# Right taps of layer 2's closing convolutions and feed-forward on VectorE, shifted copies from one plain tile

## The chip, the cores and the metric

The kernel runs as one program on one core of a Trainium2 chip. The metric is the device time of one execution in microseconds. Before the change the median of three runs is 25713.89 us (25709.84 to 25717.19).

## What is computed

The network has four layers on images of 64 channels and 64x64 pixels, batch 8. The parts concerned are in layer 2. Everything is fp32. Its last steps are, cut to what matters:

```python
y = spa_ssm(x0, ...) + x0                                   # selective scan, residual
y = dwconv3x3(gelu(dwconv3x3(y, vout_dw1)), vout_dw2) + y   # the closing convolutions
x = y + x
t = layernorm(x, ln2_g, ln2_b)
t = leaky_relu(conv1x1(t, ff_w1), 0.2)                      # 64 -> 256 channels
t = leaky_relu(dwconv3x3(t, ff_dw), 0.2)                    # depthwise, 256 channels
x = conv1x1(t, ff_w2) + x                                   # 256 -> 64 channels
```

`dwconv3x3` is a depthwise 3x3 convolution with zero padding: each output pixel of a channel is the sum of nine neighbours of the same channel, each by a weight ("tap") of that channel.

## The kernel before

Tiles are bands of 16 image rows: T = 1024 pixels. The closing convolutions (`l2_finish`) have two images on 128 partitions (a pair), NP = 4 pairs and 4 bands in each, so 16 ticks; the feed-forward (`l2_ffn`) has one image at a time, NB = 8, 32 ticks.

A strip is a padded band of 18 rows of 66 pixels for 64 channels. Its lower 64 partitions hold the band from column 1, its upper 64 partitions the same band from column 2, one pixel shifted. So one matmul over 128 partitions with a diagonal weight (`full`) adds the middle and the left tap of one row of the 3x3 window. The right tap is a second matmul over 64 partitions with the weight `right`; `conv_pair` sends the first half of the rows through the lower and the second half through the upper partitions, and two strips (e = 0, 1: two images, or two groups of 64 channels) to the two halves of the output's partitions. In one `conv_pair` there are twelve matmuls for the middle and left taps (L340), twelve for the right ones (L350), and for the second closing convolution four more that add the residual `y` through an identity (L363). The result stands in a PSUM tile of 128x1024.

`tap_diag` (L323) makes the diagonal weights on VectorE at the start of each of the two parts.

In `l2_finish` a tick t runs `fetch(t + 2)`, `first(t)`, `second(t - 1)`, in that order on every queue, as the schedule is by hand. `fetch` (L1394) loads both shifted copies of each image by DMA, half of them issued from SyncE, half from GpSimd. `first` convolves, ScalarE applies gelu for each image into the lower half of strip `mid` (L1411), GpSimd copies it to the upper half (L1412) and takes over two rows from the band before (L1414). `second` convolves `mid`, VectorE adds the layer's input `x` (L1432), and SyncE stores. At the end of an image pair `second` does one more row: GpSimd overwrites rows of `mid` (L1427, L1428) and a small convolution follows.

In `l2_ffn` a tick t convolves four groups of 64 hidden channels in two pairs (`convolve(t, j)`), and between its halves makes the hidden channels of two ticks later (`hidden(t + 2, g)`: a matmul into `pf` at L330, leaky relu by ScalarE at L1578, the shifted copy by VectorE at L1637, edge rows by GpSimd at L1639 and L1640), the norm of three ticks later (`centre`, L1615 and L1617; `scale`, L1622 to L1627) and at its end the output of the tick before (`output(t - 1)`, matmuls at L1663, VectorE's addition `xo` at L1671). The hidden matmul's weight holds each group of 64 columns twice, and only the lower half of `pf` is read. PSUM pool `pf` has one buffer, shared by `hidden` and `output`; `ps` and `pc` have two each.

Of the kernel before, what the change touches and what calls it, by code (L numbers as in the profile page):

```python
# [18 lines left out]
C = 64  # L19
HW = 64  # L20
# [86 lines left out]
def layouts(i):  # L107
# [61 lines left out]

    o["l2_f1"] = twice(np.repeat(i[p + "ff_w1"].reshape(C, 4, 1, C), 2, axis=2).reshape(C, 4, 128))  # L170
    o["l2_fd"] = twice(i[p + "ff_dw"].reshape(9, 4, C).transpose(2, 1, 0))
    o["l2_f2"] = i[p + "ff_w2"].reshape(2, 128, C).transpose(1, 0, 2)

# [75 lines left out]
class Net:  # L249
# [64 lines left out]

    def tap_diag(self, cp, names, w):

        full, right = (cp.tile([128, 3, C], F32, name=x) for x in names)
        for r in range(2):
            at = slice(r * C, r * C + C)
            for i in range(3):  # L320
                for t, j in ((full, 1 - r), (right, 2)):
                    tap = w[at, i * 3 + j : i * 3 + j + 1]
                    self.nc.vector.tensor_scalar(t[at, i, :], self.ident[at, at], tap, None, ALU.mult)  # L323
        return full, right

# [6 lines left out]
    def conv_pair(self, ps, ws, pads, r0, rows=(8, 8), term=None):  # L332


        for h, n in enumerate(rows):
            for i in range(3):
                for e in range(2):
                    o = ps[e * C : e * C + C, h * 512 : h * 512 + n * HW].rearrange("p (a b) -> p a b", b=HW)
                    f = r0 + h * 8 + i
                    self.nc.tensor.matmul(  # L340
                        o, ws[e][0][:, i, :], pads[e][0][:, f : f + n, 1 : HW + 1], start=i == 0, stop=False
                    )
            yield True
        for i in range(3):
            for h, n in enumerate(rows):
                at = slice(h * C, h * C + C)
                for e in range(2):
                    o = ps[e * C : e * C + C, h * 512 : h * 512 + n * HW].rearrange("p (a b) -> p a b", b=HW)
                    f = r0 + h * 8 + i
                    self.nc.tensor.matmul(  # L350
                        o,
                        ws[e][1][at, i, :],
                        pads[e][h][at, f : f + n, 2 : HW + 2],
                        start=False,
                        stop=i == 2 and term is None,
                    )
        if term is not None:
            for h, n in enumerate(rows):
                at = slice(h * C, h * C + C)
                for e in range(2):  # L360
                    o = ps[e * C : e * C + C, h * 512 : h * 512 + n * HW].rearrange("p (a b) -> p a b", b=HW)
                    f = term[1] + h * 8
                    self.nc.tensor.matmul(  # L363
                        o, self.ident2[at, :C], term[0][e][h][at, f : f + n, 1 : HW + 1], start=False, stop=True
                    )
        yield True
# [984 lines left out]
    def l2_finish(self, src, hy, dst):  # L1351
# [3 lines left out]
        with ExitStack() as ctx:  # L1355
# [3 lines left out]
            dw = self.load(cp, "l2_dw")  # L1359
            convs = [self.tap_diag(cp, (f"conv{j}", f"right{j}"), dw[:, j, :]) for j in range(2)]  # L1360

            def rows(name, n):
# [4 lines left out]
                return [[self.padded(t) for t in pair] for pair in flat]  # L1367


            sums, mids = rows("sum", 4), rows("mid", 2)  # L1370
            total = 4 * NP
# [8 lines left out]
            def fetch(t):  # L1380
                if t >= total:
                    return
                q, c = divmod(t, 4)
                lo, hi = max(0, c * 16 - 1), min(HW, c * 16 + 17)
                at = lo - (c * 16 - 1)
                for i in range(2):
                    s = sums[t % 4][i][0]
                    if c == 0:
                        nc.gpsimd.memset(s[:, 0, :], 0.0)
                    if c == 3:  # L1390
                        nc.gpsimd.memset(s[:, 17, :], 0.0)
                    for r in range(2):
                        engine = nc.sync if r else nc.gpsimd
                        engine.dma_start(  # L1394
                            s[r * C : r * C + C, at : at + hi - lo, 1 + r : 1 + r + HW],
                            hy[q, i * C : i * C + C, lo * HW : hi * HW].rearrange("p (a b) -> p a b", b=HW),
                        )
                xs[t] = []
                for r0, _, _, n in parts(c):
                    xs[t].append(tp.tile([128, n * HW], F32, name="x" if n > 1 else "x1"))  # L1400
                    nc.sync.dma_start(xs[t][-1], src[q, :, r0 * HW : (r0 + n) * HW])

            def first(t):
                if t >= total:
                    return
                ps = p1.tile([128, T], F32, name="ps")
                yield from self.conv_pair(ps, (convs[0],) * 2, sums[t % 4], 0)
                for i in range(2):
                    s, last = mids[t % 2][i][0], mids[(t - 1) % 2][i][0]
                    o = s[:C, 2:18, 1 : 1 + HW]  # L1410
                    nc.scalar.activation(o, like(ps[i * C : i * C + C], o), AF.Gelu)  # L1411
                    nc.gpsimd.tensor_copy(s[C:, 2:18, 2 : 2 + HW], o)  # L1412
                    if t % 4:
                        nc.gpsimd.tensor_copy(s[:, 0:2, :], last[:, 16:18, :])  # L1414
                    else:
                        nc.gpsimd.memset(s[:, 1, :], 0.0)

            def second(t):
# [3 lines left out]
                for (r0, m0, s0, n), x in zip(parts(c), xs.pop(t)):  # L1422
                    if n == 1:

                        for i in range(2):
                            s = mids[t % 2][i][0]
                            nc.gpsimd.tensor_copy(s[:, 0:2, :], s[:, 16:18, :])  # L1427
                            nc.gpsimd.memset(s[:, 2, :], 0.0)  # L1428
                    ps = p2.tile([128, T], F32, name="ps")
                    halves = (8, n - 8) if n > 8 else (n,)  # L1430
                    yield from self.conv_pair(ps, (convs[1],) * 2, mids[t % 2], m0 - 1, halves, (sums[t % 4], s0))
                    nc.vector.tensor_tensor(x, ps[:, : n * HW], x, ALU.add)  # L1432
                    nc.sync.dma_start(dst[q, :, r0 * HW : (r0 + n) * HW], x)

            with tc.manual_schedule():
                for t in range(2):
                    fetch(t)
                for t in range(total + 1):
                    fetch(t + 2)
                    for _ in first(t):  # L1440
                        pass
                    for _ in second(t - 1):
                        pass

# [135 lines left out]
    def l2_ffn(self, src, dst):  # L1580
# [6 lines left out]
        with ExitStack() as ctx:  # L1587
# [3 lines left out]
            cent2, mean2 = self.load(cp, "cent2"), self.load(cp, "mean2")  # L1591
            f1, fd, f2, g2, b2 = (self.load(cp, "l2_" + n) for n in ("f1", "fd", "f2", "g2", "b2"))
            w = [self.tap_diag(cp, (f"full{g}", f"right{g}"), fd[:, g, :]) for g in range(4)]
            flat = [[cp.tile([128, 18 * (HW + 2) + 1], F32, name=f"strip{j}{g}") for g in range(4)] for j in range(3)]
            for row in flat:
                for t in row:
# [31 lines left out]

            def hidden(t, g):
                if t >= total:  # L1630
                    return
                c = t % 4
                s, last = strips[t % 3][g][0], strips[(t - 1) % 3][g][0]
                pf = pf_.tile([128, T], F32, name="pf")
                self.sides(pf, f1[:, g, :], xn[t])
                self.leaky(s[:C, 1:17, 1 : HW + 1], pf[:C].rearrange("p (a b) -> p a b", b=HW))
                nc.vector.tensor_copy(s[C:, 1:17, 2 : HW + 2], s[:C, 1:17, 1 : HW + 1])  # L1637
                if c:
                    nc.gpsimd.tensor_copy(s[:, 0, :], last[:, 16, :])  # L1639
                    nc.gpsimd.tensor_copy(last[:, 17, :], s[:, 1, :])  # L1640
                else:
                    nc.gpsimd.memset(s[:, 0, :], 0.0)
                if c == 3:
                    nc.gpsimd.memset(s[:, 17, :], 0.0)

            def convolve(t, j):

                pc = pc_.tile([128, T], F32, name="pc")
                g = slice(2 * j, 2 * j + 2)
                yield from self.conv_pair(pc, w[g], strips[t % 3][g], 0)  # L1650
                h[t, j] = hp.tile([128, T], F32, name=f"h{j}")
                self.leaky(h[t, j], pc)
# [22 lines left out]
            with tc.manual_schedule():  # L1675
# [5 lines left out]
                for t in range(2):  # L1681
                    for g in range(4):
                        hidden(t, g)
                for t in range(total):
                    fetch(t + 4)
                    for j in range(2):
                        more = convolve(t, j)
                        for g in range(2):
                            hidden(t + 2, 2 * j + g)
                            next(more)  # L1690
                        (scale if j else centre)(t + 3)
# [285 lines left out]
```

## Time and profile before

| | us |
|---|---|
| median of the runs | 25713.89 |
| profiled execution | 25708.36 |
| its span, first to last instruction | 25706.6 |
| PE busy | 21763.6 (85%) |
| VectorE busy | 22248.8 (87%) |
| GpSimd busy | 21624.2 (84%) |
| ScalarE busy | 14830.2 (58%) |
| closing convolutions, first to last matmul | 10933.3 to 11213.3 |
| feed-forward, first matmul to last `xo` | 11219.1 to 12219.3 |

The span is the time from the first instruction to the last of one profiled execution; the runs' times contain a little around it. The busy shares are means over stages with different limits (most of the span is selective scans, which the change does not touch), so they do not tell what bounds the two parts concerned. PE, PEld, DVE, ACT and POOL are TensorE's matmuls and weight loads, VectorE, ScalarE and GpSimd. In a row of the timeline the start and the duration in us come first, then engine, line, operation, output and inputs; the bracket is the idle time before it and what ended it. In a row of groups, the numbers after the bar are the total busy us, the mean ns of one instruction, and the idle time before them.

### The profile page before, as it was taken

What the parts mean: (1) busy time and instruction counts of PE and PEld (TensorE: products, weight loads), DVE (VectorE), ACT (ScalarE), POOL (GpSimd) and SP (SyncE); (2) the same over time, 40 slices, a digit from 0 to 9 for tenths busy, and PEclk for the clock granted to TensorE, in tenths of its full rate; (3) what the DMA queues carried; (4) which work ended last, traced back from release to release, by engine and by line L of the source; (5) the groups of instructions that cost most, each with busy time, mean ns of one, the idle gap of its engine ahead of it and who ended that gap; (6) DMA issues with size and microseconds to landing.
All of it is one profiled execution on the core that took longest, in us unless ns stands there. A gap on an engine that the chain in (4) does not pass through costs nothing. (4 is left out here: it accounts for less than half of the span.)

```text
span 25706.6 us, 198113 instructions
## 1 busy us (share of the span) xinstructions
PE 21763.6 (85%) x55754; PEld 8441.0 (33%) x55754; DVE 22248.8 (87%) x12884; ACT 14830.2 (58%) x18642; POOL 21624.2 (84%) x10205
## 2 busy tenths in 40 slices
PE   8777888888888888789888888888878888888888
PEld 5522333333333223222333333333333333333333
DVE  4389989989899689922899999999989999999999
ACT  4345555555555455512666666666666666666666
POOL 0089999999999579910899999999989999999999
PEclk9888999999999999998999999999999999999999
DMA  2289899888888568830555455545545555555554
GB/s 60 79 292 318 311 316 314 309 311 316 309 312 311 186 266 325 308 62 15 161 169 170 166 172 167 170 168 168 169 155 169 168 170 169 169 168 171 167 171 157
DMA packets 1775344, 5292.32 MB, mean 206 GB/s; under 512 B 536720, under 2 KB 543060, under 8 KB 1706400
## 3 DMA queue, kind: packets, MB, share of 16 engines
q1 hardware_dynamic: 1744032, 5207.12, 59.5%
q10 hardware_dynamic: 27136, 63.34, 0.8%
q0 software_dynamic: 3072, 9.18, 0.2%
q8 instruction: 443, 7.26, 0.1%
q14 instruction: 661, 5.41, 0.1%
HBM read 5122.15 MB, written 156.11 MB: 205 GB/s over the span
## 5 line engine op out<-in xcount | busy, mean ns | idle before, releaser
L444 POOL TENSOR_TENSOR hb<-du,bc 128x1024 f32<-128x1024 f32 x4608 | 10746.5, 2356 | 495.5 <-DVE h L460 325.9
L286 PE MATMUL acc<-hc,ident 128*128 128x512 f32 x18816 | 8872.6, 613 | 90.9 <-DVE img L1207 62.3
L451 ACT ACTIVATE dA<-dt,w_A 128x512 f32<-128x512 f32 x8192 | 5662.6, 691 | 4112.6 <-DVE hc L474 3121.8
L460 DVE TENSOR_TENSOR_SCAN dA<-dA,hb 128x1024 f32<-128x1024 f32 x3384 | 7725.6, 2283 | 283.9 <-ACT dA L451 113.0
L286 PE MATMUL acc<-h,ident 128*128 128x512 f32 x7808 | 4557.9, 713 | 2350.0 <-POOL h L474 2349.9
L286 PEld LDWEIGHTS acc<-hc,ident 128*128 128x128 f32 x18816 | 3686.5, 199 | 5290.5 <-issue 4660.2
L444 POOL TENSOR_TENSOR hb<-du,b 128x1024 f32<-128x1024 f32 x2048 | 4869.5, 2403 | 487.7 <-DVE h L460 257.7
L474 DVE TENSOR_TENSOR hc<-dA,bc 128x1024 f32<-128x1024 f32 x3296 | 4035.9, 1224 | 260.5 <-issue 6.3
L451 ACT ACTIVATE dA<-dt,w_l_A 128x1024 f32<-128x1024 f32 x2560 | 2856.4, 1117 | 1178.3 <-DVE hc L474 749.9
L460 DVE TENSOR_TENSOR_SCAN dA<-dA,carry,hb 128x1024 f32<-128x1024 f32 x1320 | 3095.1, 2345 | 167.7 <-ACT carry L1190 109.6
L286 PEld LDWEIGHTS acc<-h,ident 128*128 128x128 f32 x7808 | 1547.8, 216 | 5013.8 <-POOL h L474 3146.0
L460 DVE TENSOR_TENSOR_SCAN h<-dA,hb 128x1024 f32<-128x1024 f32 x1352 | 3082.4, 2280 | 47.0 <-ACT dA L451 46.3
L474 POOL TENSOR_TENSOR h<-h,bc 128x1024 f32<-128x1024 f32 x1312 | 3088.5, 2354 | 14.2 <-DVE h L460 14.2
L474 DVE TENSOR_TENSOR hc<-dA,c 128x1024 f32<-128x1024 f32 x1408 | 1723.9, 1224 | 117.3 <-DMA c<-bc 6.2
L474 POOL TENSOR_TENSOR h<-h,c 128x1024 f32<-128x1024 f32 x640 | 1512.4, 2363 | 10.0 <-ACT carry L1190 9.6
L460 DVE TENSOR_TENSOR_SCAN h<-dA,carry,hb 128x1024 f32<-128x1024 f32 x600 | 1404.7, 2341 | 81.9 <-ACT dA L451 76.4
L451 ACT ACT_TABLE_LOAD x1122 | 1439.5, 1283 | 21.2 <-ACT tmp L976 1.2
L1190 ACT COPY carry<-dA 128x1 f32<-128x1 f32 x1056 | 167.9, 159 | 1746.1 <-DVE hc L474 1681.9
L1844 PE MATMUL mm<-xn,taps 128*128 128x512 f32 x2048 | 938.9, 600 | 33.1 <-POOL xn L1810 30.8
L673 POOL MEMSET xf<- 128x24 f32 x33 | 4.3, 141 | 910.0 <-PE ps L694 732.3
L1859 PE MATMUL mm<-u,w_xp 128*36 128x512 f32 x1024 | 518.9, 631 | 145.2 <-ACT u L1856 140.8
L1640 POOL COPY strip<-strip 128x66 f32<-128x66 f32 x96 | 22.9, 238 | 722.3 <-DVE strip L1637 696.1
(304 smaller groups left out, 19121.0 us busy)
## 6 DMA issues: line engine op xcount, KB each, us to landing
bc<-bc SPq DMA_DIRECT2D x4096, 512.0 KB
b<-bc SPq DMA_DIRECT2D x2048, 512.0 KB
c<-bc SPq DMA_DIRECT2D x2048, 512.0 KB
bc<-bc SPq DMA_DIRECT2D x512, 1024.0 KB
tmp<-rs SPq DMA_DIRECT2D x93, 512.0 KB
raw<-x SPq DMA_DIRECT2D x64, 512.0 KB
inv<-rs SPq DMA_DIRECT2D x64, 512.0 KB
tmp<-x SPq DMA_DIRECT2D x192, 128.0 KB
```

What stands on the lines that cost most here:

```text
L286: self.nc.tensor.matmul(o, lhsT, r, start=start, stop=stop)
L444: nc.gpsimd.tensor_tensor(s.shaped(hb[i]), s.shaped(s.du), B.pop(i), ALU.mult)
L451: nc.scalar.activation(dA[i][:, cut], s.dt[:, cut], AF.Exp, scale=A[:, n : n + 1])
L460: nc.vector.tensor_tensor_scan(h[:, way], dA[i][:, way], hb.pop(i)[:, way], s.first(n), ALU.mult, ALU.add)
L474: engine.tensor_tensor(s.shaped(o), s.shaped(h), CC.pop(i), ALU.mult)
L673: nc.gpsimd.memset(x[:, :, HW:], 0.0)
L1190: nc.scalar.copy(self.carry[:, n : n + 1], h[:, last : last + 1])
L1640: nc.gpsimd.tensor_copy(last[:, 17, :], s[:, 1, :])
L1844: nc.tensor.matmul(tokens(px[:, j * W : j * W + W]), taps[k][:, m, j * 128 : j * 128 + 128], xn[:, :, f : f + HW], start=m == 0, stop=m == 1,)
L1859: nc.tensor.matmul(pd, xp[:, k, j, :], u[:, j * W : j * W + W], start=j == 0, stop=j == 1)
```

## The change

The middle and left taps stay on TensorE. The right taps become three VectorE instructions on the finished PSUM tile (`right_taps`): each multiplies a window of the band by a per-channel weight and adds it to the PSUM tile in place. For that a plain tile holds 128 channels at once (two images, or two groups of hidden channels) without the shift, and GpSimd makes the two strips from it with four copies (`twin`). Weights `right` are no longer made.

In the closing convolutions `fetch` loads the plain tile `sumx` alone, in two DMAs of 128 partitions, both issued from SyncE; `spread(t + 1)` makes strips `sum` from it, one tick ahead, in GpSimd's queue before `first(t)`. There are three pairs of `sum` strips instead of four, and four plain tiles. Gelu runs once on 128 partitions into plain tile `midx`, and `twin` makes strips `mid`. Row copies are done for three tiles instead of two.

In the feed-forward a hidden step makes two groups at once, so two steps in a tick instead of four; leaky relu writes the plain tile, `twin` makes two strips, and VectorE's shifted copy goes. The first half of each convolution is now issued before the hidden step. The scalars for the right taps of two groups are loaded as `l2_fx`.

```diff
-    o["l2_f1"] = twice(np.repeat(i[p + "ff_w1"].reshape(C, 4, 1, C), 2, axis=2).reshape(C, 4, 128))
+    o["l2_f1"] = twice(i[p + "ff_w1"].reshape(C, 2, 128))
+    o["l2_fx"] = i[p + "ff_dw"].reshape(9, 2, 128).transpose(2, 1, 0)
...
+    def right_taps(self, ps, x, w, r0, n):
+        o = ps[:, : n * HW].rearrange("p (a b) -> p a b", b=HW)
+        for i in range(3):
+            self.nc.vector.scalar_tensor_tensor(
+                o, x[:, r0 + i : r0 + i + n, 2 : HW + 2], w[:, 3 * i + 2 : 3 * i + 3], o, ALU.mult, ALU.add
+            )
+
+    def twin(self, pair, x, rows):
+        for e in range(2):
+            v = x[e * C : e * C + C, rows, 1 : HW + 1]
+            for r in range(2):
+                self.nc.gpsimd.tensor_copy(pair[e][0][r * C : r * C + C, rows, 1 + r : 1 + r + HW], v)
...
-        for i in range(3):
+        for i in range(3 if right[0] is not None else 0):
...
-            sums, mids = rows("sum", 4), rows("mid", 2)
+            sums_x, mids_x = plain("sumx", 4), plain("midx", 2)
+            sums, mids = rows("sum", 3), rows("mid", 2)
...
-                    for r in range(2):
-                        engine = nc.sync if r else nc.gpsimd
-                        engine.dma_start(
-                            s[r * C : r * C + C, at : at + hi - lo, 1 + r : 1 + r + HW],
-                            hy[q, i * C : i * C + C, lo * HW : hi * HW].rearrange("p (a b) -> p a b", b=HW),
-                        )
+                for e, f in ((0, 9), (9, 18)):
+                    f0, f1 = max(lo, lo - at + e), min(hi, lo - at + f)
+                    nc.sync.dma_start(
+                        s[:, f0 - lo + at : f1 - lo + at, 1 : 1 + HW],
+                        hy[q, :, f0 * HW : f1 * HW].rearrange("p (a b) -> p a b", b=HW),
+                    )
...
+            def spread(t):
+                if t < total:
+                    self.twin(sums[t % 3], sums_x[t % 4], slice(0, 18))
...
-                for i in range(2):
-                    s, last = mids[t % 2][i][0], mids[(t - 1) % 2][i][0]
-                    o = s[:C, 2:18, 1 : 1 + HW]
-                    nc.scalar.activation(o, like(ps[i * C : i * C + C], o), AF.Gelu)
-                    nc.gpsimd.tensor_copy(s[C:, 2:18, 2 : 2 + HW], o)
+                self.right_taps(ps, sums_x[t % 4], dw[:, 0, :], 0, 16)
+                x = mids_x[t % 2]
+                o = x[:, 2:18, 1 : 1 + HW]
+                nc.scalar.activation(o, like(ps, o), AF.Gelu)
+                for s, last in zip([x] + [m[0] for m in mids[t % 2]], [mids_x[t % 2 - 1]] + [m[0] for m in mids[t % 2 - 1]]):
                     if t % 4:
                         nc.gpsimd.tensor_copy(s[:, 0:2, :], last[:, 16:18, :])
                     else:
                         nc.gpsimd.memset(s[:, 1, :], 0.0)
+                self.twin(mids[t % 2], x, slice(2, 18))
...
-                        for i in range(2):
-                            s = mids[t % 2][i][0]
+                        for s in [mids_x[t % 2]] + [m[0] for m in mids[t % 2]]:
                             nc.gpsimd.tensor_copy(s[:, 0:2, :], s[:, 16:18, :])
                             nc.gpsimd.memset(s[:, 2, :], 0.0)
...
+                    self.right_taps(ps, mids_x[t % 2], dw[:, 1, :], m0 - 1, n)
                     nc.vector.tensor_tensor(x, ps[:, : n * HW], x, ALU.add)
...
                 for t in range(total + 1):
                     fetch(t + 2)
+                    spread(t + 1)
+                    first(t)
+                    second(t - 1)
...
-                self.leaky(s[:C, 1:17, 1 : HW + 1], pf[:C].rearrange("p (a b) -> p a b", b=HW))
-                nc.vector.tensor_copy(s[C:, 1:17, 2 : HW + 2], s[:C, 1:17, 1 : HW + 1])
+                o = v[:, 1:17, 1 : HW + 1]
+                self.leaky(o, like(pf, o))
+                self.twin(pair, v, slice(1, 17))
...
                 yield from self.conv_pair(pc, w[g], strips[t % 3][g], 0)
+                self.right_taps(pc, plain[t % 3][j], fx[:, j, :], 0, 16)
...
                         more = convolve(t, j)
-                        for g in range(2):
-                            hidden(t + 2, 2 * j + g)
-                            next(more)
+                        next(more)
+                        hidden(t + 2, j)
+                        next(more)
                         (scale if j else centre)(t + 3)
```

More of the change, by code (lines that the diff above doesn't have):

```diff
@@ L313, in folded, with tap_diag @@
         return full, right
-    def tap_diag(self, cp, names, w):
-        full, right = (cp.tile([128, 3, C], F32, name=x) for x in names)
+    def tap_diag(self, cp, name, w):
+        t = cp.tile([128, 3, C], F32, name=name)
         for r in range(2):
@@ L320, in tap_diag @@
             for i in range(3):
[L321 to L324, printed above, removed]
+                tap = w[at, i * 3 + 1 - r : i * 3 + 2 - r]
+                self.nc.vector.tensor_scalar(t[at, i, :], self.ident[at, at], tap, None, ALU.mult)
+        return t
+    def right_taps(self, ps, x, w, r0, n):
[9 more added lines that the diff above has]
+                self.nc.gpsimd.tensor_copy(pair[e][0][r * C : r * C + C, rows, 1 + r : 1 + r + HW], v)
     def sides(self, ps, lhsT, rhs, start=True, stop=True):
@@ L332, in conv_pair @@
     def conv_pair(self, ps, ws, pads, r0, rows=(8, 8), term=None):
+        full, right = zip(*ws)
         for h, n in enumerate(rows):
@@ L340, in conv_pair @@
                     self.nc.tensor.matmul(
-                        o, ws[e][0][:, i, :], pads[e][0][:, f : f + n, 1 : HW + 1], start=i == 0, stop=False
+                        o,
+                        full[e][:, i, :],
+                        pads[e][0][:, f : f + n, 1 : HW + 1],
+                        start=i == 0,
+                        stop=i == 2 and right[e] is None and term is None,
                     )
             yield True
-        for i in range(3):
+        for i in range(3 if right[0] is not None else 0):
             for h, n in enumerate(rows):
@@ L351, in conv_pair @@
                         o,
-                        ws[e][1][at, i, :],
+                        right[e][at, i, :],
                         pads[e][h][at, f : f + n, 2 : HW + 2],
@@ L1359, in l2_finish @@
             dw = self.load(cp, "l2_dw")
-            convs = [self.tap_diag(cp, (f"conv{j}", f"right{j}"), dw[:, j, :]) for j in range(2)]
+            convs = [(self.tap_diag(cp, f"conv{j}", dw[:, j, :]), None) for j in range(2)]
             def rows(name, n):
@@ L1367, in rows, with plain @@
                 return [[self.padded(t) for t in pair] for pair in flat]
-            sums, mids = rows("sum", 4), rows("mid", 2)
+            def plain(name, n):
+                flat = [cp.tile([128, 18, HW + 2], F32, name=f"{name}{j}") for j in range(n)]
+                for t in flat:
+                    nc.gpsimd.memset(t, 0.0)
+                return flat
+            sums_x, mids_x = plain("sumx", 4), plain("midx", 2)
+            sums, mids = rows("sum", 3), rows("mid", 2)
             total = 4 * NP
@@ L1385, in fetch @@
                 at = lo - (c * 16 - 1)
-                for i in range(2):
[L1387 to L1391, printed above, removed]
-                    for r in range(2):
-                        engine = nc.sync if r else nc.gpsimd
-                        engine.dma_start(
-                            s[r * C : r * C + C, at : at + hi - lo, 1 + r : 1 + r + HW],
-                            hy[q, i * C : i * C + C, lo * HW : hi * HW].rearrange("p (a b) -> p a b", b=HW),
-                        )
+                s = sums_x[t % 4]
+                if c == 0:
+                    nc.gpsimd.memset(s[:, 0, :], 0.0)
+                if c == 3:
+                    nc.gpsimd.memset(s[:, 17, :], 0.0)
+                for e, f in ((0, 9), (9, 18)):
[4 more added lines that the diff above has]
+                    )
                 xs[t] = []
@@ L1406, in first @@
                 ps = p1.tile([128, T], F32, name="ps")
-                yield from self.conv_pair(ps, (convs[0],) * 2, sums[t % 4], 0)
-                for i in range(2):
-                    s, last = mids[t % 2][i][0], mids[(t - 1) % 2][i][0]
-                    o = s[:C, 2:18, 1 : 1 + HW]
-                    nc.scalar.activation(o, like(ps[i * C : i * C + C], o), AF.Gelu)
-                    nc.gpsimd.tensor_copy(s[C:, 2:18, 2 : 2 + HW], o)
+                for _ in self.conv_pair(ps, (convs[0],) * 2, sums[t % 3], 0):
+                    pass
+                self.right_taps(ps, sums_x[t % 4], dw[:, 0, :], 0, 16)
[3 more added lines that the diff above has]
+                for s, last in zip([x] + [m[0] for m in mids[t % 2]], [mids_x[t % 2 - 1]] + [m[0] for m in mids[t % 2 - 1]]):
                     if t % 4:
@@ L1423, in second @@
                     if n == 1:
-                        for i in range(2):
-                            s = mids[t % 2][i][0]
+                        for s in [mids_x[t % 2]] + [m[0] for m in mids[t % 2]]:
                             nc.gpsimd.tensor_copy(s[:, 0:2, :], s[:, 16:18, :])
@@ L1430, in second @@
                     halves = (8, n - 8) if n > 8 else (n,)
-                    yield from self.conv_pair(ps, (convs[1],) * 2, mids[t % 2], m0 - 1, halves, (sums[t % 4], s0))
+                    for _ in self.conv_pair(ps, (convs[1],) * 2, mids[t % 2], m0 - 1, halves, (sums[t % 3], s0)):
+                        pass
+                    self.right_taps(ps, mids_x[t % 2], dw[:, 1, :], m0 - 1, n)
                     nc.vector.tensor_tensor(x, ps[:, : n * HW], x, ALU.add)
@@ L1437, in l2_finish @@
                     fetch(t)
+                spread(0)
                 for t in range(total + 1):
                     fetch(t + 2)
[L1440 to L1443, printed above, removed]
+                    spread(t + 1)
+                    first(t)
+                    second(t - 1)
     def l2_scan(self, hx, hy):
@@ L1591, in l2_ffn @@
             cent2, mean2 = self.load(cp, "cent2"), self.load(cp, "mean2")
-            f1, fd, f2, g2, b2 = (self.load(cp, "l2_" + n) for n in ("f1", "fd", "f2", "g2", "b2"))
-            w = [self.tap_diag(cp, (f"full{g}", f"right{g}"), fd[:, g, :]) for g in range(4)]
+            f1, fd, fx, f2, g2, b2 = (self.load(cp, "l2_" + n) for n in ("f1", "fd", "fx", "f2", "g2", "b2"))
+            w = [(self.tap_diag(cp, f"full{g}", fd[:, g, :]), None) for g in range(4)]
             flat = [[cp.tile([128, 18 * (HW + 2) + 1], F32, name=f"strip{j}{g}") for g in range(4)] for j in range(3)]
-            for row in flat:
+            plain = [[cp.tile([128, 18, HW + 2], F32, name=f"plain{j}{g}") for g in range(2)] for j in range(3)]
+            for row in flat + plain:
                 for t in row:
@@ L1627, in scale, with hidden @@
                     nc.vector.tensor_scalar(o, o, g2, b2, ALU.mult, ALU.add)
-            def hidden(t, g):
+            def hidden(t, j):
                 if t >= total:
@@ L1632, in hidden @@
                 c = t % 4
-                s, last = strips[t % 3][g][0], strips[(t - 1) % 3][g][0]
+                v, pair = plain[t % 3][j], strips[t % 3][2 * j : 2 * j + 2]
                 pf = pf_.tile([128, T], F32, name="pf")
-                self.sides(pf, f1[:, g, :], xn[t])
-                self.leaky(s[:C, 1:17, 1 : HW + 1], pf[:C].rearrange("p (a b) -> p a b", b=HW))
-                nc.vector.tensor_copy(s[C:, 1:17, 2 : HW + 2], s[:C, 1:17, 1 : HW + 1])
[L1638 to L1644, printed above, removed]
+                self.sides(pf, f1[:, j, :], xn[t])
+                o = v[:, 1:17, 1 : HW + 1]
+                self.leaky(o, like(pf, o))
+                self.twin(pair, v, slice(1, 17))
+                before = plain[(t - 1) % 3][j], *(p[0] for p in strips[(t - 1) % 3][2 * j : 2 * j + 2])
+                for s, last in zip((v, *(p[0] for p in pair)), before):
+                    if c:
+                        nc.gpsimd.tensor_copy(s[:, 0, :], last[:, 16, :])
+                        nc.gpsimd.tensor_copy(last[:, 17, :], s[:, 1, :])
+                    else:
+                        nc.gpsimd.memset(s[:, 0, :], 0.0)
+                    if c == 3:
+                        nc.gpsimd.memset(s[:, 17, :], 0.0)
             def convolve(t, j):
@@ L1681, in l2_ffn @@
                 for t in range(2):
-                    for g in range(4):
-                        hidden(t, g)
+                    for j in range(2):
+                        hidden(t, j)
                 for t in range(total):
```

## The prediction

> **What bounds the kernel now.** Nearly all of the span lies in parts the change leaves alone; first I asked which stretches hold it. The page's groups and the tiles `sum`, `mid` and `strip` place layer 2's closing convolutions from 10905 to 11220 us and its feed-forward from 11220 to 12230. The table of windows tells what each is made of:
>
> ```profile
> 10905.00:11220.00 315.00, 282.71 (x1785) 91.64 (x1786) 29.49 (x45) 34.96 (x34) 89.52 (x143) 0.94 0.62 121
> 11220.00:12230.00 1010.00, 881.15 (x3970) 245.75 (x3968) 314.29 (x346) 240.46 (x261) 63.28 (x269) 0.88 0.07 16
> 11057.30:11074.24 16.94, 16.94 (x109) 5.20 (x105) 1.23 (x1) 2.04 (x2) 4.36 (x6) 1.00 0.68 132
> 11715.86:11746.60 30.74, 27.64 (x128) 7.69 (x124) 9.36 (x10) 7.42 (x8) 1.67 (x8) 0.89 0.00 1
> ```
>
> After the stretch and its length come PE, PEld, DVE, ACT and POOL, then granted clock, DMA share and GB/s. One closing tick (third row, 16.94 us) has PE busy all through at full clock: TensorE is the bound. A feed-forward tick (last row, 30.74) has 3.1 us without PE and a clock of 0.89, so something else ends last. The timeline of that tick shows what:
>
> ```profile
> 11712.06 1.12 PE L1622 MATMUL ps<-xn,w_mean 128*128 128x512 f32 x2
> 11713.12 2.81 PE L350 MATMUL pc<-strip,right 64*64 64x512 f32 x24
> 11713.29 0.69 ACT L1624 ACTIVATE xn<-ps,eps 128x512 f32<-128x512 f32 x1 [2.75 <-PE ps L1622]
> 11714.01 3.35 DVE L1625 RECIPROCAL xn<-xn 128x512 f32<-128x512 f32 x1 [2.75 <-ACT xn L1624]
> ...
> 11718.70 2.05 DVE L1671 TENSOR_TENSOR xo<-pf,x 64x512 f32<-64x512 f32 x2
> 11720.90 2.08 PE L330 MATMUL pf<-xn,w_l_f 64*128 64x512 f32 x4 [3.10 <-DVE xo L1671]
> 11722.90 4.83 PE L340 MATMUL pc<-strip,full 128*64 128x512 f32 x12
> ```
>
> Output and hidden layer share one PSUM buffer `pf`, so the next `pf` matmul waits for VectorE's `xo`, which stands behind the reciprocal. After the 3.10 us gap L330 takes 2.08 (1.13 elsewhere) and a half convolution 4.83 (2.80 elsewhere): the clock is halved. Thus the loop is: `L1622` at 12.06 to `pf` at 20.87, 8.81 us; then PE's own queue back to `L1622` at 42.80.
>
> **Durations.** For the new operations I took these rows:
>
> ```profile
> L795 DVE SCALAR_TENSOR_TENSOR g<-q,w_l_bv,g 128x512 f32<-128x512 f32 x32 | 23.9, 747 | 25.2 <-ACT g L791 25.2
> L1432 DVE TENSOR_TENSOR x<-ps,x 128x1024 f32<-128x1024 f32 x12 | 14.7, 1225 | 180.5 <-PE ps L363 180.5
> L1412 POOL COPY mid<-mid 64x1024 f32<-64x1024 f32 x32 | 33.1, 1035 | 136.8 <-ACT mid L1411 135.8
> L1626 DVE TENSOR_TENSOR xn<-ps,xn 128x512 f32<-128x512 f32 x32 | 22.1, 692 | 1.1
> ```
>
> A tap is a scalar_tensor_tensor of 1024 columns: 747 ns plus the 533 by which a tensor_tensor grows from 512 to 1024 columns (1225 - 692) is 1.28 us, with a gap of 0.04 between dependent VectorE operations (as between the reciprocal and L1626), so 1.32, and 3.96 for three. No row writes PSUM from VectorE. Below, 1.22 (the tensor_tensor row) is the floor; above, I allow double, 2.6, if reading and writing PSUM took turns. I take 1.32.
>
> **The skill.** In the Trainium skill, "VectorE: DVE Perf Modes", section on the perf-mode tier table, fp32 tensor_tensor and any PSUM operand run one element per cycle; the 1225 ns row agrees. "PSUM — Partial Sum Buffer", Specifications, lets VectorE write 4-byte data to PSUM and read one tensor from it; no run here shows such a write. "GPSIMD Engine Reference", Key points, has GpSimd share SBUF interfaces with VectorE operations in a 2-port mode or with two SBUF inputs. The trace agrees: 64x64 tensor_scalars (L323) last about 1.03 us beside GpSimd's memsets and 0.24 after them. A tap has one SBUF tensor and one in PSUM, so it should neither slow the copies nor be slowed. "TensorE: Matmul & The Clock Gate", What's actually happening, halves the clock after an idle window of about 3.4 us and restores it after a busy one; the slow stretch above, some 5.8 us, fits.
>
> **Closing convolutions, steady.** Each tick loses two blocks of right taps: 2.74 (11071.50 to 11074.24) and 2.63 (11062.60 to 11065.23), 5.37 in all; PE keeps 5.30 + 5.30 + 0.97 = 11.57 us. Does anything else need longer? VectorE: six taps and an add, 7.92 + 1.23 = 9.2. GpSimd: four copies of 64x1152 at 1.035 x 1152/1024, 4.66; four of 64x1024, 4.14; three row copies, 0.9; 9.7. ScalarE: one gelu, 1.02, where two were. DMA: the sum loads halve from 4 half-partition transfers to 2 full ones; 0.68 of 16.94 is 11.5 us before, about 7 after (estimate by packets and bytes). SP's sums and x cost about as much to issue, and GpSimd's own issues (about 0.87 each) go. So 11.57 stays PE's. Latency: first convolution, three taps (3.96), gelu (1.1), four copies (4.14), ending 14.6 us into the tick; its reader is due at 11.57 + 5.3 = 16.9. Slack 2.3. SP's loads for two ticks ahead land near 14, due at 16. 16 x 5.37 = 86 us gross.
>
> **What eats it.** At an image pair's end (4 times) the one-row part needs GpSimd to overwrite rows of `midx`, which now waits for the taps that read them; PE queues behind. Taps 3.96 and copies 1.2 leave PE idle 5.3 us (before: 0.9), the clock halves, and some 6.5 us of work at half rate costs 3.3. Against the former extra of 1.1 (18.05 - 16.94) the new is about 9.4: 8.3 x 4 = 33. At the start second(0) waits for taps, gelu with its table load, and copies: idle 5.4 and another slow stretch, 8; at the end second(15) and its taps, 3. The memsets grow from 12 to 16 (4.4 us), but the GpSimd loads that stood behind them are gone; even. 86 - 33 - 11 = 42 us.
>
> **Feed-forward, steady.** PE loses two right blocks (5.5) and two of four `pf` blocks (2.1), but PE is not the bound: the loop counts. Its part to `pf` gains three taps, since convolve(t,1)'s taps stand on VectorE behind scale's operations and ahead of `xo`: 8.81 + 3.96 = 12.8. The rest loses a right block and two `pf` blocks, and full00 moves ahead of the wait: `pf` 2.03 and half convolution 4.76 at half clock, L1615 1.05, half 2.73, `pf` 1.06, half 2.73: 14.4. Sum 27.2 against 30.72. PE stalls about 7 us in each. Work elsewhere: VectorE 14.6, GpSimd 8.3 + 2.9 (its copies end about 5 us into the next loop, read later), ScalarE 5.4: all covered. The lost 64x1024 VectorE copy was not in the loop. From the second to the 29th tick (11327.23 to 12145.88, 818.7) I get 27 x 27.2 = 734: 84 us.
>
> **Start and tail.** Half of 48 weight products go, some 4.5 us (they run beside the memsets); eight hidden steps of 3.26 become four, 13: 17.8 with rounding. Six more memsets end before their first reader. The first two ticks, 50.6, lose about 12: less PE work, no `pf` wait in the first. Of the last three, one keeps the loop without the centre step (28.6 to 25.2) and two are PE alone (17.8 to 12.6 each): 13.8; the last taps before the last `xo` cost 2. Sum: 84 + 17.8 + 12 + 11.8 = 126 us.
>
> **Total.** 42 + 126 = 168. The profiled execution took 25708.36 (span 25706.6), which gives 25540; the median, 25713.89, lies 5.5 above, so 25546.
>
> **Rivals.**
> 1. Taps dear (about 2.3 us each). Loop 8.81 + 7 + 14.4 = 30.2; closing ticks become VectorE's, 6 x 2.34 + 1.23 = 15.3, and image ends give the rest back. Only start and tail remain, about 50: 25665. For it: no row writes PSUM from VectorE. Against: PSUM reads cost nothing extra per column.
> 2. GpSimd becomes the closing bound: if its copies slow 1.5 times under VectorE, 14.5 us a tick; the saving there goes, net 125: 25590. Against: layer 1's L875 copies keep 1035 ns beside scans.
> 3. No half-clock stretch in the feed-forward: the loop is 24.1, 80 more: 25465. The first ticks before (27.63 apart) ran so, but at a 3 us stall; 7 us speaks against it.
> 4. Slower: taps over the break-even. The feed-forward loop gains nothing at (30.72 - 23.2)/3 = 2.5 us a tap; closing breaks even earlier. At 2.8 the loop costs 31.6 (+25), closing ticks 18 (+17) and image ends (+40), less 30 at start and tail: about +50, 25765.
> 5. The right taps stay on PE or the order is not as read: the PE queue of the changed program holds no matmul on `right`, so I give it nothing.
>
> **Chances.** Mine 0.72, rival 1 0.10, 2 0.08, 3 0.05, 4 0.05. The main case alone runs from 25500 (clock lost for less time) to 25590 (image ends and stalls dearer). Leaving out rival 4 and most of 1 and 3, the range is 25495 to 25620. About 0.2% (51 us) is what a measurement of this kernel can tell from no change. Faster takes mine, 2, 3 and most of 1: 0.91; 0.04 same; 0.05 slower.
>
> **What would show it.** Taps of 1.25 to 1.35 us; closing ticks near 11.6 with four PE gaps of 5 us before 128x64 matmuls; feed-forward ticks near 27.2 with the `pf` matmul still released by `xo`, PE idle 7 us; GpSimd copies at 1.03 us. Taps above 2 us, copies above 1.4, or `pf` released by another engine would make me wrong.

## The result and the profile after

The changed kernel takes 25495.61 us in the median of four runs (25494.33 to 25501.22); the kernel before, on the same chip, 25715.54 (25709.84 to 25727.59). The ratio is 0.9914, 95% interval 0.9897 to 0.9931: faster by 0.86%, some 220 us, where 168 were forecast. The median lies at the lowest edge of the range; the ratio applied to 25713.89, the median that the forecast started from, gives 25493, 2 us below it. The profiled execution took 25501.22 (span 25499.4), 207 less than that of before; it was the slowest of its four runs, while that of before was faster than all four of its own, so the profiles hold 13 us less than the medians.

The table of windows of the changed kernel is laid out as that of before: the two parts, then one tick of each (the stretch and its length, PE, PEld, DVE, ACT and POOL, granted clock, DMA share, GB/s).

```profile
10905.00:11167.00 262.00, 206.19 (x970) 65.76 (x970) 152.24 (x141) 18.70 (x18) 174.92 (x227) 0.89 0.41 110
11167.00:12020.00 853.00, 620.21 (x2176) 174.57 (x2174) 467.28 (x383) 171.50 (x195) 352.45 (x659) 0.83 0.08 19
10972.78:10984.25 11.47, 11.47 (x60) 3.53 (x56) 8.90 (x7) 1.02 (x1) 9.50 (x12) 1.00 0.56 139
11605.93:11632.33 26.40, 19.26 (x69) 5.44 (x69) 14.27 (x11) 5.28 (x6) 10.49 (x21) 0.87 0.00 1
```

A closing tick is still TensorE without a gap, 11.47 us in place of 16.94. A feed-forward tick is still one that TensorE does not fill: 26.40 in place of 30.74, with 7.1 us of idle time. The timeline of that tick has the same chain, with the taps (L330) in it:

```profile
11604.87 1.12 PE L1658 MATMUL ps<-xn,w_mean 128*128 128x512 f32 x2
...
11606.75 3.35 DVE L1661 RECIPROCAL xn<-xn 128x512 f32<-128x512 f32 x1 [5.39 <-ACT xn L1660]
...
11611.33 4.00 DVE L330 SCALAR_TENSOR_TENSOR pc<-plain,w_l_fx,pc 128x1024 f32<-128x1024 f32 x3
11615.36 2.07 DVE L1712 TENSOR_TENSOR xo<-pf,x 64x512 f32<-64x512 f32 x2
...
11617.58 2.08 PE L345 MATMUL pf<-xn,w_l_f 64*128 64x512 f32 x4 [7.14 <-DVE xo L1712]
11619.58 4.20 PE L357 MATMUL pc<-strip,full 128*64 128x512 f32 x12
...
11643.98 2.08 PE L345 MATMUL pf<-xn,w_l_f 64*128 64x512 f32 x4 [7.13 <-DVE xo L1712]
11645.98 4.64 PE L357 MATMUL pc<-strip,full 128*64 128x512 f32 x12
```

From scale's matmul (11604.87) to the `pf` matmul (11617.58) it is 12.71 us, where before it was 8.84 (11712.06 to 11720.90; the forecast's 8.81 counts to the weight load, 0.03 us earlier). The half convolution after the wait, slow in both, takes 4.20 in this tick and 4.64 in the next; before it took 4.83. The groups of the new operations (the mean ns of one follows the busy us):

```profile
L330 DVE SCALAR_TENSOR_TENSOR pc<-plain,w_l_fx,pc 128x1024 f32<-128x1024 f32 x192 | 247.2, 1288 | 211.1 <-PE pc L357 201.2 <-ACT h L1612 1.1 <-DVE pc L330 0.5
L339 POOL COPY strip<-plain 64x1024 f32<-64x1024 f32 x256 | 266.3, 1040 | 462.2 <-ACT plain L1612 454.1
```

A tap lasts 1.29 us and a copy 1.04, though they run beside each other.

Where the 207 us between the profiles went is read at two points, the first feed-forward matmul (11219.07 before) and the end of the last `xo` (12219.25 before). After the change they are:

```profile
11166.38 2.04 PE L1651 MATMUL ps<-x,w_cent 128*128 128x512 f32 x2 [4.87 <-DMA w_cent<-in_cent_dram]
...
12008.32 2.08 DVE L1712 TENSOR_TENSOR xo<-pf,x 64x512 f32<-64x512 f32 x2 [3.82 <-PE pf L1704]
```

The closing convolutions gave 53, the feed-forward 156 (1000.2 to 844.0), and the rest of the span moved by 2 the other way.

### The profile page after: what moved, and what is told of

It is laid out like the page before. It is cut to its first block, busy times and chain, and to the rows that moved or that the text cites. A ratio compares the mean times of both kernels' runs of the same rounds, so it can differ in the third digit from the quotient of the medians.

```text
span 25499.4 us, 193264 instructions
## 1 busy us (share of the span) xinstructions
PE 21439.3 (84%) x53146; PEld 8356.0 (33%) x53146; DVE 22515.7 (88%) x13020; ACT 14749.0 (58%) x18562; POOL 22003.6 (86%) x10679
## 5 line engine op out<-in xcount | busy, mean ns | idle before, releaser
L339 POOL COPY strip<-plain 64x1024 f32<-64x1024 f32 x256 | 266.3, 1040 | 462.2 <-ACT plain L1612 454.1
```

The costliest lines, as they stand in the source:

```text
L339: self.nc.gpsimd.tensor_copy(pair[e][0][r * C : r * C + C, rows, 1 + r : 1 + r + HW], v)
```

## The experiments

The theory: two independent gains, TensorE's queue in the closing part and the loop through `xo` in the feed-forward; what the forecast mis-sized is how long TensorE runs at half clock after the wait for `xo`, and what holds TensorE at an image pair's end. Each ratio is to the kernel before on that run's chip. Unless another comparison is named, a difference is taken from the changed kernel's ratio; each ratio's interval is some 40 us either way, so such a difference is good to about 60, and the traces are named where they tell more.

**Each part alone.** The closing convolutions as changed with the feed-forward of before, which makes its `right` weights again (cut to a few lines):

```diff
-    o["l2_f1"] = twice(i[p + "ff_w1"].reshape(C, 2, 128))
+    o["l2_f1"] = twice(np.repeat(i[p + "ff_w1"].reshape(C, 4, 1, C), 2, axis=2).reshape(C, 4, 128))
...
-                self.twin(pair, v, slice(1, 17))
...
+                nc.vector.tensor_copy(s[C:, 1:17, 2 : HW + 2], s[:C, 1:17, 1 : HW + 1])
...
-                self.right_taps(pc, plain[t % 3][j], fx[:, j, :], 0, 16)
```

> The closing convolutions as changed, the feed-forward as before. If the two parts add up as the two profiles lay them out (the first feed-forward matmul stands 52.7 us earlier after the change than before it), the span falls by about 53 us, 0.2%. If the gain of one part leans on the other, or some of the 207 us between the two profiles lies outside both parts, it differs from that by more than 10 us.

It took 25645.81 us, ratio 0.9973 (0.9962 to 0.9984), about 69 us less than before; its profile has the first feed-forward matmul at 11164.7, 54 us earlier than before, and its span is 52 us shorter. The interval (41 to 98 us) holds the 53 expected but is too wide to tell 10 us more or less; the trace agrees with the 53 to about 1 us.

The other way round (again cut):

```diff
-            sums_x, mids_x = plain("sumx", 4), plain("midx", 2)
-            sums, mids = rows("sum", 3), rows("mid", 2)
...
+            sums, mids = rows("sum", 4), rows("mid", 2)
...
-                self.right_taps(ps, sums_x[t % 4], dw[:, 0, :], 0, 16)
...
+                    nc.gpsimd.tensor_copy(s[C:, 2:18, 2 : 2 + HW], o)
...
-                    self.right_taps(ps, mids_x[t % 2], dw[:, 1, :], m0 - 1, n)
```

> The feed-forward as changed, the closing convolutions as before. By the two profiles the feed-forward, from its first matmul to its last addition, takes 156 us less: I expect 150 to 160 us less in all, with ticks of 26.4 us in the mean. If the feed-forward's gain came partly from a clock phase inherited from the faster closing part, ticks would lie elsewhere, between 25.5 and 27.3 us.

It took 25553.6 us, ratio 0.9936 (0.9922 to 0.9951), 165 us less; in its profile the feed-forward lasts 845 us, with ticks of 26.4 us in the mean, as in the changed kernel. So neither gain leans on the other by more than a few us, and no third part of the kernel is needed to explain the result.

**Is `xo` behind the taps what sets the tick?** VectorE's addition ahead of the second pair's taps:

```diff
                         (scale if j else centre)(t + 3)
+                        if j:
+                            output(t - 1)
                         for _ in more:
                             pass
-                    output(t - 1)
```

> The output step's addition xo is issued ahead of the second pair's three taps on VectorE; TensorE's order is unchanged. Theory: the loop that sets a feed-forward tick runs from scale's matmul through VectorE to xo and the pf matmul, so taking three taps of 1.32 us off it lowers the part up to pf from 12.7 to 8.75 us, and the tick to 20.1 us at full clock, 20.1 to 23.2 with a slow stretch: 90 to 170 us off the span. Rival (GpSimd's four copies or ScalarE's order hold the hidden step, not xo): the tick stays above 25 us.

It took 25363.78 us, ratio 0.9862 (0.9845 to 0.9878), 134 us under the changed kernel's; by the traces the feed-forward takes 722 us in place of 844. Two ticks of its timeline, one after which the clock halves and one after which it does not:

```profile
11503.61 1.12 PE L1658 MATMUL ps<-xn,w_mean 128*128 128x512 f32 x2
...
11510.19 2.06 DVE L1712 TENSOR_TENSOR xo<-pf,x 64x512 f32<-64x512 f32 x2
...
11512.40 2.08 PE L345 MATMUL pf<-xn,w_l_f 64*128 64x512 f32 x4 [3.21 <-DVE xo L1712]
...
11525.33 1.12 PE L1658 MATMUL ps<-xn,w_mean 128*128 128x512 f32 x2
...
11534.11 1.13 PE L345 MATMUL pf<-xn,w_l_f 64*128 64x512 f32 x4 [3.20 <-DVE xo L1712]
```

From scale's matmul to `pf` is now 8.79 us. Ticks lie between 20.2 and 22.9 us, 21.7 in the mean, within the stated 20.1 to 23.2. The taps were in the loop: the part up to `pf` fell by 3.9 us, about what three taps take (4.0). The tick fell by 4.7, since behind these waits of 3.1 to 3.2 us TensorE runs at half clock for less time, and in some ticks not at all.

**What does the half clock cost?** In the 7 us wait TensorE gets matmuls into the half of `pc` that the convolution overwrites later, so the result stays the same. `warm(t, n)` issues 2n of them, each with a 128x64 weight and 512 columns:

```diff
                         next(more)
+                        if j == 0 and 0 < t < total - 2:
+                            warm(t, 14)
                         hidden(t + 2, j)
```

> 28 matmuls more in each of 29 feed-forward ticks, in the 7 us in which TensorE waits for xo, into PSUM columns that the convolution overwrites after: the result stays the same, TensorE only has something to do. Theory (after the stall the clock is halved for 3.0 to 6.3 us, which costs a tick 2.4 us in the mean): the tick falls from 26.4 to 24.1 us and the span by about 60 us, though TensorE does more work. Rival (the stretch after the stall is slow for another reason, such as the operands or PSUM): no change, or slower by what the added matmuls overrun.

It took 25574.59 us, ratio 0.9944 (0.9929 to 0.9959): 77 us more than the changed kernel, where 60 less were expected. The filler was mis-sized: 28 matmuls take 12.2 us, 5 more than the wait. The clock in a tick of 28.87 us is 1.00 all the same. With half of them, in the same place:

```diff
-                            warm(t, 14)
+                            warm(t, 7)
```

> The filler again, with 14 matmuls in place of 28: the 28 took 12.2 us, 0.435 each, and overran the wait of 7.1 us by 5; 14 take 6.1 and end before xo. The result stays the same. Theory (idle TensorE halves its clock after the stall, 2.4 us a tick in the mean): tick 24.1 us, the span about 60 us under the changed kernel's. Rival (the slow stretch has another cause, or the added matmuls cost elsewhere): tick 26.4 or more.

It took 25433.44 us, ratio 0.9892 (0.9877 to 0.9907): 57 us under the changed kernel's, with more work on TensorE; by the traces the feed-forward takes 780 us in place of 844. Its table of windows, for one tick, and its timeline (which has two entries for a matmul, so x28 are the 14):

```profile
11419.49:11443.45 23.96, 22.93 (x97) 6.86 (x96) 14.21 (x11) 5.28 (x6) 10.00 (x21) 1.00 0.04 12
```

```profile
11495.73 6.18 PE L1702 MATMUL pc<-strip,full 128*64 128x512 f32 x28
11502.93 1.13 PE L345 MATMUL pf<-xn,w_l_f 64*128 64x512 f32 x4 [1.02 <-DVE xo L1723]
11503.99 2.80 PE L357 MATMUL pc<-strip,full 128*64 128x512 f32 x12
```

The tick is 23.96 us at clock 1.00, and none is longer than 24.1. `pf` still waits for `xo`, so the loop is the same, and what follows runs at full speed: the changed kernel's half clock costs 26.4 - 24.0 = 2.4 us a tick, not the 3.0 of the forecast (2.03 + 4.76 in place of 1.06 + 2.73).

**What holds TensorE at an image pair's end?** In the changed kernel's timeline TensorE waits 4.60 us before the one-row part's 128x64 matmuls, then runs at half clock (7.81 us for a convolution that takes 5.37):

```profile
11101.66 1.09 PE L384 MATMUL ps<-sum,ident 64*64 64x512 f32 x8
11101.77 4.27 POOL L339 COPY mid<-midx 64x1024 f32<-64x1024 f32 x4 [2.00 <-ACT midx L1443]
11102.92 3.94 DVE L330 SCALAR_TENSOR_TENSOR ps<-midx,w_l_dw,ps 128x1024 f32<-128x1024 f32 x3 [2.35 <-PE ps L384]
11106.10 0.29 POOL L1459 COPY midx<-midx 128x132 f32<-128x132 f32 x1
...
11106.92 0.15 POOL L1460 MEMSET midx<- 128x66 f32 x1 [0.52 <-DVE ps L330]
...
11107.35 1.22 PE L357 MATMUL ps<-mid,conv 128*64 128x64 f32 x12 [4.60 <-POOL mid L1459]
...
11108.92 7.81 PE L357 MATMUL ps<-sum,conv 128*64 128x512 f32 x24
```

The row copies start right behind GpSimd's four copies of the next band, not behind the taps; only the memset of `midx` between them waits for the taps, 0.52 us. To tell the two apart, only `midx` is left alone (`right_taps` gets the number of taps as an argument):

```diff
-                        for s in [mids_x[t % 2]] + [m[0] for m in mids[t % 2]]:
+                        for s in [m[0] for m in mids[t % 2]]:
                             nc.gpsimd.tensor_copy(s[:, 0:2, :], s[:, 16:18, :])
                             nc.gpsimd.memset(s[:, 2, :], 0.0)
...
-                    self.right_taps(ps, mids_x[t % 2], dw[:, 1, :], m0 - 1, n)
+                    self.right_taps(ps, mids_x[t % 2], dw[:, 1, :], m0 - 1 if n > 1 else 16, n, 3 if n > 1 else 2)
```

> At an image pair's end the one-row part's taps read the last two rows of midx where they stand (the third row is zero and is left out), so GpSimd no longer overwrites rows of midx; it still does so for the two strips. As the prediction has it (GpSimd's copy waits for the main part's taps, TensorE queues behind it), the wait before the 128x64 matmuls falls from 4.6 to about 1.2 us and the clock stays up: 25 us less. Rival (in the trace GpSimd is busy with the same tick's copies into mid until 0.1 us before the row copies, so these would be as late without the taps): the wait falls to 3.8 us, 3 us less in all.

It took 25491.29 us, ratio 0.9915 (0.9901 to 0.993), no different from the changed kernel. By the traces its closing part is 4 us shorter (229.2 against 233.3), and in its timeline the wait is 3.71 us:

```profile
11104.33 1.23 PE L357 MATMUL ps<-mid,conv 128*64 128x64 f32 x12 [3.71 <-POOL mid L1459]
```

The rival holds: GpSimd's queue, not the taps, makes up most of this wait. Then without any row copies (`conv_pair` and `right_taps` both take the number of rows of the window that are left, and the one-row part starts at row 16):

```diff
-                    if n == 1:
-                        for s in [mids_x[t % 2]] + [m[0] for m in mids[t % 2]]:
-                            nc.gpsimd.tensor_copy(s[:, 0:2, :], s[:, 16:18, :])
-                            nc.gpsimd.memset(s[:, 2, :], 0.0)
...
+                    f0, taps = (m0 - 1, 3) if n > 1 else (16, 2)
```

> The one-row part reads rows 16 and 17 of strips and plain tile where they stand, in matmuls and taps, and GpSimd overwrites nothing; the third row is zero and is left out. Both theories of the row copies give the same here: TensorE goes on without a wait, 4.6 us and the slow stretch after it saved at each of four ends, 25 to 32 us less in all. If the slow stretch after an image end had another cause than the wait, 18 us.

It took 25471.4 us, ratio 0.9907 (0.9892 to 0.9922): 18 us less by the ratios. From the first closing matmul to the first of the feed-forward the traces say 209.8 us (10923.43 to 11133.27) against 233.3 (10933.05 to 11166.38): 23.5 less. The medians cannot tell the 18 of the wait alone from the 25 to 32 with the slow stretch; the trace lies nearer the second.

**Both together.** The image ends as in the last run, and the feed-forward reordered so that neither the reciprocal nor the second taps stand between an output and its `xo`. `deviate` is scale's matmul and square root, `scale` what is left, its part on VectorE:

```diff
                 for t in range(total):
                     fetch(t + 4)
-                    for j in range(2):
-                        more = convolve(t, j)
-                        next(more)
-                        hidden(t + 2, j)
-                        next(more)
-                        (scale if j else centre)(t + 3)
-                        for _ in more:
-                            pass
+                    more = convolve(t, 0)
+                    next(more)
                     output(t - 1)
+                    next(more)
+                    hidden(t + 2, 0)
+                    deviate(t + 3)
+                    for _ in more:
+                        pass
+                    scale(t + 3)
+                    more = convolve(t, 1)
+                    next(more)
+                    hidden(t + 2, 1)
+                    next(more)
+                    centre(t + 4)
+                    for _ in more:
+                        pass
```

> The image ends as in the run before, and in the feed-forward another order: the output step between the two halves of the first pair's convolution, so that xo stands behind no reciprocal; scale's matmul and square root in the first pair of a tick, its VectorE part behind the first taps; the centre step, one tick earlier, in the second pair. Theory: no wait of TensorE is left, it is the bound at four half convolutions of 2.73, two pf blocks of 1.06, centre and scale of 1.05 and an output of 1.94: 17.1 us a tick at full clock, 28 x 9.3 = 260 us less, with the image ends 290 us: about 25205 us. Rival (VectorE, 14.6 us of work in a tick in an order of dependences, becomes the bound): ticks of 19 to 21 us and half to three quarters of it.

It took 25239.31 us, ratio 0.9817 (0.98 to 0.9833): 470 us under the kernel before and some 250 under the changed one. One tick, by the table of windows, and the wait that is left, by the timeline:

```profile
11480.58:11498.19 17.61, 16.92 (x70) 4.83 (x68) 14.43 (x12) 5.39 (x6) 10.62 (x23) 1.00 0.05 16
```

```profile
11499.15 1.02 ACT L1608 ACTIVATE h<-pc 128x1024 f32<-128x1024 f32 x1 [2.88 <-DVE pc L330]
11500.22 1.08 PE L1705 MATMUL pf<-h,w_l_f 128*64 128x512 f32 x4 [1.00 <-ACT h L1608]
```

TensorE is busy 16.9 of 17.6 us at full clock, and all steady ticks lie between 17.6 and 18.2, under the rival's 19 to 21. The output now comes soon after the taps that make its input, so it waits 0.7 to 1.25 us for `h`, 0.9 in the mean: some 26 of the 40 us that the expectation had in excess. By the traces the feed-forward gave 237 us of the 260 expected (844.0 to 607.3), the closing part 23 of the 30.

## Why the prediction was right and where it was off

**Direction, bounds and most durations: right.** A tap was put at 1.28 and measured 1.29, so here VectorE's reading and writing of PSUM in one instruction costs nothing beyond the forecast's price, in which a column costs what it does in a tensor_tensor; rivals 1 and 4 fall. GpSimd's copies kept 1.04 us beside the taps, so rival 2 falls. The closing tick was forecast at 11.57 and is 11.47. The part of the feed-forward loop up to `pf` was forecast at 12.8 and is 12.71 in the tick shown and 12.63 in the mean, with the wait ended by `xo` as before, and the run with `xo` ahead of the taps shows the three taps in it.

**The step that failed: "`pf` 2.03 and half convolution 4.76 at half clock".** It carried the slow stretch of before, about 6 us, into every tick. The loop was forecast at 27.2; from the second to the 29th tick it is 26.39 in the mean (11237.16 to 11949.66), 22 us less over 27 ticks. Of these, 16 are this step: `pf` and the half convolution together take 6.20 us in the mean where 6.79 stood. The part up to `pf` gave 4 (12.63 where 12.77 stood), and 2 are the rounding of 27.13 to 27.2. It is the largest of the terms that missed; the others follow below.

One can read from the timeline when the full clock came back. A half convolution takes 2.73 us at full clock, so one that takes d until the next block starts ran the first x = 2 (d - 2.73) us at half clock. For the tick above d is 4.13 (11619.58 to 11623.71), so the clock came back at 11622.38; in the next d is 4.58 and it came back at 11649.68, 27.30 us later. The table of windows, cut at these points, has the granted clock itself (after the five engines' times) and agrees within 0.07 us:

```profile
11615.61:11622.44 6.83, 4.87 (x12) 1.53 (x14) 1.79 (x2) 1.80 (x2) 1.62 (x2) 0.50 0.01 4
11622.44:11639.51 17.07, 14.40 (x58) 3.91 (x54) 10.11 (x8) 3.23 (x4) 8.94 (x19) 1.00 0.00 0
11639.51:11649.75 10.24, 5.78 (x14) 1.77 (x16) 4.15 (x4) 2.05 (x2) 2.43 (x3) 0.50 0.50 103
```

The Trainium skill, "TensorE: Matmul & The Clock Gate", What's actually happening, says that the activity window is 3413 ns and free-running; 27.30 is eight of these. All through the feed-forward the clock falls and returns on such a grid, with the returns seven or eight windows apart, and so the slow stretch from the start of `pf` varies from 3.0 to 6.4 us and is 5.0 in the mean. In the kernel before the ticks from 11444 us on are 30.7 us in the mean, and nine windows are 30.72, so the loop met the same point of the grid every time and paid 6.1 to 6.3 us. The length that the forecast carried over belonged to that tick, not to the wait. Rival 3 (no slow stretch, 24.1) is the other end: the run with 14 filler matmuls has it, 23.96.

The skill's section also has the clock fall after an idle window of about 3.4 us. Here less was enough. In the kernel before:

```profile
11354.98:11358.39 3.41, 1.82 (x8) 0.37 (x8) 3.34 (x4) 1.02 (x1) 0.00 (x0) 1.00 0.00 0
11358.39:11361.81 3.42, 2.05 (x10) 0.74 (x12) 1.22 (x2) 0.83 (x1) 0.00 (x0) 1.00 0.00 0
...
11716.79:11720.21 3.42, 1.00 (x6) 0.12 (x2) 3.29 (x5) 0.23 (x1) 0.00 (x0) 1.00 0.00 0
11720.21:11727.03 6.82, 6.13 (x14) 1.77 (x16) 1.23 (x2) 1.02 (x1) 0.42 (x2) 0.50 0.00 0
```

In the first two rows an early wait of 2.96 us (11356.80 to 11359.76) is split between two windows, 1.59 us of idle TensorE in one and 1.37 in the other, and the clock stays full. In the third, 2.42 us of a wait of 3.10 (11717.79 to 11720.90) fall into one window, and the clock is halved at its end. In the feed-forward ticks of the seven traces in which the clock falls there, it fell only after a window with at least 1.9 us of idle TensorE and stayed full after none with more than 2.0; it came back after windows with at most 0.40 us idle and stayed halved after those with 0.41 or more. So a wait of some 3 us halves the clock or not by where it lies on the grid. The 7 us wait of the changed kernel always did, and what varied was the return.

**Closing part, 42 forecast, 53 measured.** The costs were put too high. An image end takes 8.3 us more than two normal ticks (31.28 - 2 x 11.47; 11091.21 to 11122.49), 7.2 net of the former 1.1, where 8.3 net stood (from 9.4, of which 5.3 and 3.3 were accounted for): 4.4 us over four ends, if the last is like the others. From the first matmul to the third tick's convolution before takes 30.5 us and after 28.3, where an even balance was forecast. Of the 4 us of the difference that are left, about 1.4 are the other 14 ticks, 0.10 shorter each than forecast; the rest lies by subtraction in the tail, which no run tests.

**The reason given for the image end was wrong.** "GpSimd ... waits for the taps ... TensorE queues behind it" has nearly the right size (5.3 forecast, 4.60 measured) but mostly the wrong cause: with `midx` left alone the wait fell only from 4.60 to 3.71. That the size came out near was luck. GpSimd's copies of the next band ended within a microsecond of the taps (11106.04 and 11106.86), and the forecast looked at the taps alone.

**Start of the feed-forward, 30 forecast, 37 measured:** to the first half convolution 22.3 us less (57.6 to 35.2) where 17.8 stood (its terms, 13 and 4.5, add up to 17.5), and 15.0 for the first two ticks (50.6 to 35.6) where 12 stood. The weight products gave their 4.5. But nine `pf` blocks stood ahead of the first half convolution (11248.31 to 11276.64), not eight, and four stand there now (11191.12 to 11201.61), since the change issues that half ahead of its tick's hidden step: 17.8 us less, not 13. Why the first two ticks gave 3 us more is open. The tail gave 12.6, forecast at 11.8.

All four terms (closing part, steady ticks, start and tail of the feed-forward) missed to the same side. The main case's fast end, 25500, allowed for a clock lost for less time, and the range left 5 us below it for gains in all other terms together.

## What to carry to other kernels

When a removed piece of work belongs to an engine that waits in every tick, price the loop through the last wait, not the engine's queue: here a tick lost 7.6 us of TensorE's work and gained 4 us of VectorE's in the loop, and moving one VectorE addition ahead of the taps was worth more than half of the change itself. A clock that falls in a wait has a cost that depends on where the loop meets the clock's own windows, so bound it from none to the longest seen rather than carry one measured stretch over. When something waits for two things that end close together, take each away before naming one.

## What the runs showed that I had not expected

- In the feed-forward the clock changed only at points 3.413 us apart, and it fell after as little as 1.9 us of idle TensorE between two of them. From 11444 us on the ticks of the kernel before were locked to nine of these windows; those of the changed kernel went through a pattern of about 25.4, 26.4, 26.8 and 27.1 us.
- Filling a 7.1 us wait with 6.1 us of needless matmuls made the kernel 57 us faster (64 in the feed-forward, by the traces).
- In the last run, a 128x512 tensor_scalar that had taken 0.55 us took 1.32 where it fell beside GpSimd's copies, while the taps beside them kept their length.
